# Node-score softmax turned through DRAM instead of TensorE, and x1 written over x

## The chip, the cores and the metric

The kernel runs on one core of one Trainium2 chip. The metric is device time in microseconds (us) of one launch. Before the change three runs took 2731.12, 2731.03 and 2728.78 us, so the median is 2731.03 us. All arithmetic is in float32.

## What is computed

The input is a batch of 64 graphs of 256 nodes with 512 features (x), their weighted adjacency matrices (256 x 256) and a node mask. Layer 0 is a three-step graph convolution with a residual and a layer norm; layer 1 is a graph attention in which each node gets one score, and the scores of a graph go through one softmax over its 256 nodes.

```python
x0 = relu(adj @ (x  @ W1) + b1)
x0 = relu(adj @ (x0 @ W2) + b2)
x1 = layernorm(x + adj @ (x0 @ W3) + b3)
q, k = split(x1 @ Wqk);  v = x1 @ Wv
w = sum_d(q * (adj @ (k * mask))) * mask / sqrt(512)      # one score per node
out = layernorm(x1 + softmax(w, over the 256 nodes)[:, None] * v)
```

## The kernel before, in words

The 64 graphs are worked on as 32 pairs (G = 2, NPAIR = 32). A graph's 256 nodes fill the 128 partitions twice (NH = 2 halves h). Every matrix product is done as seven smaller products of half-size blocks instead of eight (`seven`, L108), so each product needs sums and differences of blocks, made by VectorE (DVE), GpSimd (POOL) or ScalarE (ACT); `unit` (L65) chooses between DVE and POOL by the list ON_DVE (L36). One such product is seven steps on TensorE (PE).

A pair goes through these stages, each written as a Python generator that yields after every step:

- **F** (`front`, L416): x @ W1 (`support`, L293; matmuls at L301), adj times that (`aggregate`, L324; matmuls at L342), the same for W2, and x0 @ W3. In its course it issues the load of the next pair's transposed x (L73) and, near its end, of this pair's plain x (`load_x`, L85 to L90).
- **S** (`sums`, L426): the block sums of the next pair's transposed x (`a_sums` with the names x7, x6, x5, x3) and of its adjacency, and x + b3 (L437).
- **B** (`back`, L442): adj times (x0 @ W3) plus x (matmuls at L378), layer norm of the sum into x1 (called `r`), a masked copy `xm` (L471), and x1 transposed by 32 x 32 blocks on DVE (L498) and two DMA stages through DRAM (`via`, L502 and L504). In the last pair PE does this transpose (L487).
- **G** (`gather`, L512): adj times the masked x1 (L378).
- **M** (`attention`, L525): the 28 steps of x1 @ (Wq Wk^T) and x1 @ Wv (matmuls at L556), whose weights are fetched from DRAM through a ring of seven buffers (`fetch`, L221; DMA at L226), and the node scores: four instructions (L573) that multiply and sum along a row, each of which fills one column of the small tile `w` (128 partitions x 4 scores).
- **E** (`finish`, L604): the softmax of the scores, v * s + x1 (L613, four instructions), the second layer norm and the store (L634).

Pair i's stages run in three consecutive rounds of the outer loop (L667): F in round i, B, G and M in round i + 1, E in round i + 2. Within a round, a string of letters (ORDER; START, LAST and END for the first and last rounds) says which generator takes its next step. `manual_schedule` (L45) makes this the order of instructions on every engine's queue: no instruction passes another one of its own engine, and that holds for the DMAs too, which are all issued by SyncE (SP). In the trace the engine PE also shows as PEld, its weight loads, which run beside the matmuls.

The **softmax** is in `softmax_rows` (L390) and `softmax_cols` (L405). A softmax over nodes runs across partitions, so the scores are first turned: two PE transposes (L395) put the two graphs' scores as two rows of 256 into a PSUM bank. DVE takes the negated maximum (L397), ACT the exponential with its sum (L400, which makes ACT load another function table first), DVE the reciprocal and the product (L402, L403) into the tile `e_t`. Two PE matmuls with the identity (L409; each is two instructions in float32) turn the rows back to columns in another PSUM bank, and DVE copies them to the tile `s` (L412), which L613 reads. E's first step is up to L403, its second from L409 to L613.

**Buffers**: the tiles x and xm share one buffer (tag x) and r has its own (tag r); each is 8 KB on each of the 128 partitions. A tile that is given a buffer waits until the last reader of the tile before it is done. x1 of pair i (r) lives until L613 of round i + 2.

Of the kernel before, what the change touches and what calls it, by code (L numbers as in the profile page):

```python
# [9 lines left out]
FP = mybir.dt.float32  # L10
AF = mybir.ActivationFunctionType
OP = mybir.AluOpType
AX = mybir.AxisListType

P = 128
PAIR = 2
G = PAIR
# [3 lines left out]
def gcn_then_graph_attention(ctx: ExitStack, tc: tile.TileContext, xT, xN, adjT, mask, W1, b1, W2, b2, W3, b3,  # L21
                             WqT, WkT, Wv, out):

    nc = tc.nc
    NPAIR = xT.shape[0]
    N, D = 256, 512
    NH, DC = N // P, D // P
# [5 lines left out]
    SBUFS = 6  # L33
    SEEDS = 2
    TMP = 5
    ON_DVE = ('a3', 'a5', 'a6', 'a7', 'b3', 'c1T5', 'c1T6', 'c1T7', 'c2T5', 'c2T6', 'c2T7', 'c3T7', 'h17', 'h23', 'h25', 'h26', 'h27')  # L36

    const = ctx.enter_context(tc.tile_pool(name="const", bufs=1))
    pool = ctx.enter_context(tc.tile_pool(name="work", bufs=1))
    small = ctx.enter_context(tc.tile_pool(name="small", bufs=2))  # L40
    dram = ctx.enter_context(tc.tile_pool(name="dram", bufs=2, space=bass.MemoryType.DRAM))
# [5 lines left out]
    def bank(shape=(P, G, N)):  # L47
        return psum.tile(list(shape), FP, name="ps", tag="ps")
# [36 lines left out]
    def load_x(i):  # L85
        k = small.tile([P, NH, G], FP, name="mask")
        nc.sync.dma_start(k, mask[i].rearrange("p (h g) -> p h g", h=NH))
        t = pool.tile([P, G, NH, D], FP, name="x", tag="x", bufs=1)
        nc.sync.dma_start(t, xN[i].rearrange("p (g h f) -> p g h f", g=G, h=NH))
        return t, k  # L90

# [75 lines left out]
    ident = const.tile([P, P], FP, name="ident")  # L167
# [14 lines left out]
    begin, end = load_w(W1, 1, True)  # L182
# [5 lines left out]
    for n, b in ((1, b1), (2, b2)):  # L188
        t = const.tile([P, DC], FP, name=f"b{n}")
# [38 lines left out]

    def make_m():

        wq = pool.tile([P, DC, D], FP, name="wqT", tag="r", bufs=1)
        wk = pool.tile([P, DC, D], FP, name="wkT", tag="T", bufs=1)
        for d in range(DC):
            for t, w in ((wq, WqT), (wk, WkT)):
                nc.sync.dma_start(t[:, d], w[d * P:(d + 1) * P, :])
        m = pool.tile([P, 2, 2, D], FP, name="m", tag="v", bufs=1)
        v = pool.tile([P, 2, 2, D], FP, name="wv", tag="gt", bufs=1)
        nc.sync.dma_start(v, Wv.rearrange("(k c p) f -> p k c f", k=2, p=P))
        yield
        for f in range(DC):  # L240
            pt = bank((P, D))
            for d in range(DC):
                for j in range(DC):
                    nc.tensor.matmul(pt[:, j * P:(j + 1) * P], lhsT=wq[:, d, f * P:(f + 1) * P],
                                     rhs=wk[:, d, j * P:(j + 1) * P], start=(d == 0 and j == 0),
                                     stop=(d == DC - 1), skip_group_check=True)
            nc.scalar.copy(m[:, f // 2, f % 2, :], pt)
            yield
        t12 = pool.tile([P, 2, 2, D], FP, name="t12", tag="r", bufs=1)
        t34 = pool.tile([P, 2, 2, D], FP, name="t34", tag="T", bufs=1)  # L250
        sub = OP.subtract

        for o, a, b, op in ((t12[:, 0], v[:, 0], m[:, 0], sub), (t12[:, 1], m[:, 1], t12[:, 0], OP.add),
                            (t34[:, 0], m[:, 1], m[:, 0], sub), (t34[:, 1], v[:, 1], t12[:, 1], sub)):
            for c in range(2):
                nc.vector.tensor_tensor(o[:, c], a[:, c], b[:, c], op=op)
                yield
        B = {1: v[:, 0], 2: v[:, 1], 3: m[:, 1], 4: t34[:, 1], 5: t12[:, 0], 6: t12[:, 1], 7: t34[:, 0]}
        at = {n: k for k, n in enumerate(INNER)}
        for q, outer in enumerate(OUTER):  # L260
            for k, n in enumerate(outer):
                w = pool.tile([P, 7, HD], FP, name="w7", tag=("Za", "Ia")[place[n] % 2], bufs=1)
                blk = [B[n][:, c, j * HD:(j + 1) * HD] for c in range(2) for j in range(2)]
                for i, b in ((1, blk[0]), (2, blk[2]), (3, blk[3])):
                    nc.scalar.copy(w[:, at[i]], b)
                yield from b_steps(blk, [w[:, at[i]] for i in (5, 6, 7, 4)], nc.vector)
                nc.sync.dma_start(w_dram[q][:, :, k], w)
                yield
        for k in range(RING):
            fetch(k)  # L270
# [116 lines left out]
        nc.vector.reciprocal(rs, sd)  # L387
        return rs

    def softmax_rows(w, gs):  # L390

        n = len(gs)
        pw = bank((n, N))
        for h in range(NH):
            nc.tensor.transpose(pw[:, h * P:(h + 1) * P], w[:, h, gs[0]:gs[0] + n], ident)  # L395
        nmax = small.tile([n, 1], FP, name="nmax")
        nc.vector.tensor_reduce(nmax, pw, AX.X, OP.max, negate=True)  # L397
        e = e_t[:n]
        tot = small.tile([n, 1], FP, name="tot")
        nc.scalar.activation(e, pw, AF.Exp, bias=nmax, accum_out=tot)  # L400
        rtot = small.tile([n, 1], FP, name="rtot")
        nc.vector.reciprocal(rtot, tot)  # L402
        nc.vector.tensor_scalar(e, e, rtot, None, op0=OP.mult)  # L403

    def softmax_cols(gs):  # L405
        n = len(gs)
        ps = bank((P, NH, n))
        for h in range(NH):
            nc.tensor.matmul(ps[:, h, :], lhsT=e_t[:, h * P:(h + 1) * P], rhs=ident[:, :n],  # L409
                             start=(h == 0), stop=(h == NH - 1), skip_group_check=True)  # L410
        s = small.tile([P, NH, n], FP, name="s", bufs=2)
        nc.vector.tensor_copy(s, ps)  # L412
        return s
# [26 lines left out]
            yield from adj_sums(aTs[i + 1], put)  # L440

    def back(i, C, aS, x, mask_t, end, put):  # L442
        r = pool.tile([P, G, NH, D], FP, name="r", tag="xT" if end else "r", bufs=1)
        xb = lambda h, j: x[:, :, h, j * HD:(j + 1) * HD]
        rb = lambda h, j: r[:, :, h, j * HD:(j + 1) * HD]
        st = small.tile([P, NH, G, 6], FP, name="st")
# [14 lines left out]
        nc.vector.tensor_scalar(ms, mask_t, ISCALE, None, op0=OP.mult)  # L461
        rs = inv_std(mvt)
        yield
        xm = pool.tile([P, G, NH, D], FP, name="xm", tag="x", bufs=1)

        def turn(h, g):
            nc.vector.tensor_scalar(r[:, g, h, :], r[:, g, h, :], mvt[:, h, g, 0:1], rs[:, h, g:g + 1],
# [51 lines left out]
                        aTs[i + 2] = load_adj(i + 2)  # L519
                yield  # L520
        put["G"] = gather()
        w = small.tile([P, NH, G], FP, name="w", bufs=2)
        put["M"] = attention(i, x1b, w, r, mask_t, put)

    def attention(i, x1b, w, r, mask_t, put):  # L525
# [45 lines left out]
        def score(R, h, g):  # L571
            t = put["gt"][:, h, g, :]
            nc.vector.scalar_tensor_tensor(t, R[:, g].rearrange("p j f -> p (j f)"), mask_t[:, h, g:g + 1], t,  # L573
                                           op0=OP.mult, op1=OP.mult, accum_out=w[:, h, g:g + 1])

        def results(g):

# [26 lines left out]
    def finish(i, prev, gs=range(G)):  # L604

        r, v, w = prev
        n = len(gs)
        softmax_rows(w, gs)
        yield
        s = softmax_cols(gs)  # L610
        for k, g in enumerate(gs):
            for h in range(NH):
                nc.vector.scalar_tensor_tensor(v[:, g, h], v[:, g, h], s[:, h, k:k + 1], r[:, g, h, :],  # L613
                                               op0=OP.mult, op1=OP.add)
        yield
        st = small.tile([P, NH, n, 6], FP, name="st")
        mvt = small.tile([P, NH, n, 2], FP, name="mvt")
        for k, g in enumerate(gs):
            for h in range(NH):
                nc.vector.bn_stats(st[:, h, k], v[:, g, h])  # L620
                yield
        for k in range(n):
            for h in range(NH):
                nc.vector.bn_aggr(mvt[:, h, k], st[:, h, k])  # L624
        rs = inv_std(mvt, n)
        nb = small.tile([P, NH, n], FP, name="nb")
        nc.vector.scalar_tensor_tensor(nb, mvt[:, :, :, 0], -1.0, rs, op0=OP.mult, op1=OP.mult)  # L627
        yield
        for k, g in enumerate(gs):
            for h in range(NH):  # L630
                nc.scalar.activation(v[:, g, h], v[:, g, h], AF.Identity, scale=rs[:, h, k:k + 1],  # L631
                                     bias=nb[:, h, k:k + 1])
                yield
            nc.sync.dma_start(out[i, :, g * NH * D:(g + 1) * NH * D].rearrange("p (h f) -> p h f", h=NH), v[:, g])  # L634

    ORDER = ("BBFEFFBBEFBBFBFBFFFFFBFFFFBFBBBFFFBFSEBGGFSGGEFEEGFMSGMFMGMFMFMFMMMEMMFMFMMMSMFEEESM"
             "SMEMFEFSEFMMMFMSMMMMSMMMMMMMMSMMMMSMMMF")
    START = ("BBFFFFFBBFFBBBBBFFFFFFFBBBBBFSFBBBBSBBBFBBBBBFBBBBBBBFBBFFFFFFBSFFFFSBBBBBBFSFBFBSBS"
             "BBFBBSFSSBSBBBBBBBBBBBFBBBSBB")
    LAST = ("FFBEBFBBEBBFFBSFBFFFEFFBSFSFFBFBFFBBFBBEEFGEEEGFGGFGFMMFMGFMFMFGMFMEEMMMMFMFFMMMSSEM"  # L640
            "SMSFMSEMMFSFMMMMMEMFMMMMMMMMMMFMMSMMMSM")
    END = ("BBBBBBBBBBBEBBBBGGEMGGMEMBGEEEBGMMMMEMMMMEMEMMEEEBMMMMMMGMMMMMMMMMMMMMMMMXMMXXMMXYMX"
           "YMYXMXMXYXYMMXMMYYYYXYYMXMY")

    def run(order, rest, **gens):
        res = {}
# [81 lines left out]
```

## Time and profile before

| | us |
|---|---|
| median of the three runs | 2731.03 |
| the profiled execution | 2725.27 |
| its span (first to last instruction) | 2723.5 |
| time around the span (difference of these two) | 1.77 |
| PE busy | 2694.6 |
| DVE busy | 2118.6 |
| ACT busy | 1278.4 |
| POOL busy | 925.5 |

The mean granted clock of TensorE was 0.996. The DMA queues moved 403.72 MB.

How to read the views that follow. In the *timeline* each row is a start in us from the start of the span, a duration, an engine, a source line, an operation with what it writes and reads, and how many instructions the row joins; a bracket at the end gives the engine's idle time before it and what ended that. PE instructions are pipelined, so a row overlaps the next one: the cost of a row of matmuls is the distance from its start to the start of the next row. In the *waits* a row names the instruction that waited and what it waited for, and then the sum in us, the number of times, and the longest. In the list of *DMA issues* the last number is the median time in us from issue to landing. "The order" is the sequence of instructions on each engine in the built program, with their waits; it has no times in it.

### The profile page before, as it was taken

Reading aid. Unit: us, or ns where it says so; the run is one execution under the profiler, and the core shown is the slowest. Engines: PE = TensorE matmul, PEld = TensorE weight load, DVE = VectorE, ACT = ScalarE, POOL = GpSimd, SP = SyncE. Lnnn points to the kernel's source line nnn. Section 1 sums busy time; section 2 is a strip of 40 time slices with the busy share of each in tenths; the row PEclk is TensorE's granted clock in tenths of the full one; section 3 lists DMA queues with packets and bytes.
Section 4 is the critical chain, followed back from the end, with each engine's and each line's share of the span. In section 5 each row is a group of like instructions: output and inputs, shape, how many; then the busy total and the mean of one; then the engine's idle time right before and its main releaser. Section 6 shows DMA issues by size and latency. Waiting matters only on the chain. (4 is left out here: it accounts for less than half of the span.)

```text
span 2723.5 us, 41056 instructions
## 1 busy us (share of the span) xinstructions
PE 2694.6 (99%) x14306; PEld 2410.4 (89%) x14306; DVE 2118.6 (78%) x3700; ACT 1278.4 (47%) x2338; POOL 925.5 (34%) x678
## 2 busy tenths in 40 slices
PE   9999999999999999999999999999999999999996
PEld 8888888888898888888888988889888889888885
DVE  5777777878777887777787778877787877787777
ACT  3534455444554444454444554444544445444444
POOL 2422343322434223433224442234332244322332
PEclk9999999999999999999999999999999999999998
DMA  5534554345544445543455444455434454444552
GB/s 199 170 123 149 165 166 137 123 149 162 165 140 131 137 149 165 174 136 116 152 158 165 142 132 136 146 164 178 135 117 152 154 164 148 136 132 146 160 157 99
DMA packets 202235, 403.72 MB, mean 148 GB/s; under 512 B 24752, under 2 KB 61872, under 8 KB 193968
## 3 DMA queue, kind: packets, MB, share of 16 engines
q1 hardware_dynamic: 202032, 401.10, 46.8%
q8 instruction: 117, 1.92, 0.3%
q14 instruction: 86, 0.70, 0.1%
HBM read 328.54 MB, written 72.48 MB: 147 GB/s over the span
## 5 line engine op out<-in xcount | busy, mean ns | idle before, releaser
L556 PE MATMUL ps<-ring,I 128*128 128x256 f32 x1792 | 434.8, 380 | 3.4 <-DVE seed L57 1.8
L66 POOL TENSOR_TENSOR S<-hT,S 128x512 f32<-128x512 f32 x64 | 93.1, 1454 | 1005.3 <-DVE S L66 1005.3
L556 PEld LDWEIGHTS ps<-ring,I 128*128 128x128 f32 x1792 | 332.5, 190 | 47.3 <-issue 4.4
L301 PE MATMUL ps<-w_T,S 128*128 128x256 f32 x1536 | 352.5, 379 | 0.0
L113 ACT COPY tmp<-ps 128x512 f32<-128x512 f32 x512 | 287.2, 588 | 123.3 <-PE ps L301 60.9
L301 PEld LDWEIGHTS ps<-w_T,S 128*128 128x128 f32 x1536 | 289.1, 190 | 39.4
L122 ACT COPY seed<-ps 128x512 f32<-128x512 f32 x256 | 146.1, 571 | 307.9 <-PE ps L301 167.4
L66 POOL TENSOR_TENSOR sup<-sup 128x512 f32<-128x512 f32 x64 | 81.8, 1298 | 589.3 <-DVE sup L66 589.3
L57 DVE TENSOR_TENSOR sup<-ps,tmp 128x512 f32<-128x512 f32 x192 | 131.5, 685 | 156.4 <-PE ps L301 155.9
L301 PE MATMUL ps<-w_T,hT 128*128 128x256 f32 x1024 | 236.7, 379 | 0.0
L63 POOL TENSOR_TENSOR I<-Z 128x384 f32<-128x384 f32 (+1 forms) x128 | 191.0, 1513 | 123.5 <-DVE Z L537 105.0
L66 DVE TENSOR_TENSOR sup<-sup 128x512 f32<-128x512 f32 x224 | 219.5, 981 | 10.3 <-DVE sup L57 0.5
L556 PE MATMUL ps<-ring,Z 128*128 128x256 f32 x896 | 219.5, 379 | 0.0
L301 PEld LDWEIGHTS ps<-w_T,hT 128*128 128x128 f32 x1024 | 194.6, 190 | 26.5
L57 DVE TENSOR_TENSOR R<-ps,tmp 128x512 f32<-128x512 f32 (+1 forms) x256 | 153.4, 621 | 74.2 <-PE ps L556 65.9
L342 PE MATMUL ps<-aS,sup 128*128 128x128 f32 x1536 | 203.3, 279 | 0.0
L342 PEld LDWEIGHTS ps<-aS,sup 128*128 128x128 f32 x1536 | 193.4, 191 | 10.4 <-DVE hT L57 2.0
L342 PEld LDWEIGHTS ps<-aT,sup 128*128 128x128 f32 x1536 | 194.4, 192 | 6.6
L342 PE MATMUL ps<-aT,sup 128*128 128x128 f32 x1536 | 199.3, 276 | 0.0
L556 PEld LDWEIGHTS ps<-ring,Z 128*128 128x128 f32 x896 | 167.7, 190 | 21.8 <-DVE tmp L57 0.4
L301 PE MATMUL ps<-w,S 128*128 128x256 f32 x768 | 182.8, 381 | 2.5 <-DVE sup L57 2.5
L565 ACT COPY R<-seed 128x512 f32<-128x512 f32 (+1 forms) x128 | 66.5, 545 | 242.0 <-PE seed L556 242.0
(135 smaller groups left out, 5407.2 us busy)
## 6 DMA issues: line engine op xcount, KB each, us to landing
ring<-mv SPq DMA_DIRECT2D x672, 256.0 KB, 3.5
x<-in_xN SPq DMA_DIRECT2D x32, 1024.0 KB, 5.2
out<-v SPq DMA_DIRECT2D x64, 512.0 KB, 3.5
xT<-in_xT SPq DMA_DIRECT2D x31, 1024.0 KB, 4.8
via<-tr SPq DMA_DIRECT2D x31, 1024.0 KB, 4.2
x1T<-via SPq DMA_DIRECT2D x124, 256.0 KB, 4.6
ring<-mv SPq DMA_DIRECT2D x224, 128.0 KB, 2.7
aT<-in_adjT SPq DMA_DIRECT2D x32, 512.0 KB, 3.6
```

The costliest lines, as they stand in the source:

```text
L57: nc.vector.tensor_tensor(o, a, b, op=OP.add)
L63: (nc.gpsimd).tensor_tensor(o, a, b, op=op)
L66: (nc.vector if name in ON_DVE else nc.gpsimd).tensor_tensor(o, a, b, op=op)
L113: nc.scalar.copy(t, ps)
L122: nc.scalar.copy(y, x)
L301: nc.tensor.matmul(ps[:, g], lhsT=src[n][:, c, g], rhs=w[n][:, c], start=(first and g == 0 and c == 0), stop=(g == G - 1 and c == 1), skip ...
L342: nc.tensor.matmul(ps[:, c, g], lhsT=C[n][:, g, c * P:(c + 1) * P], rhs=aS[n][:, g], start=(first and c == 0 and g == 0), stop=(c == 1 and ...
L556: nc.tensor.matmul(ps[:, k], lhsT=left[n](place[o]), rhs=wt[:, k], start=(first and k == 0), stop=(k == len(outer) - 1), skip_group_check= ...
L565: return seven(mm, (P, len(outer), HD), lambda y: nc.scalar.copy(R[:, :, 0, 0], y), c12, lambda v, t: add(R[:, :, 1, 0], v, t), lambda v, ...
```

## The change

For the first 31 pairs (the last pair's graphs are finished one at a time and keep the PE path) the softmax no longer uses PE or PSUM. The scores are written from `w` to DRAM, element by element in row order (`wr`), read back as two rows of 256 (`row`), put through the same softmax in place, written to DRAM again (`sr`), and read back as columns into `s`. E gains steps for this: one for each of the four DMAs and one for the row arithmetic. The tile `w` changes its order from (h, g) to (g, h) so that the DMA's pattern is plain.

x1 is written in place over x (r = x), the tag r goes, and tag x has two buffers; xm takes its buffer from tag x too (in the last pair from tag xT). The two set-up tiles that used tag r use tag x.

Two of the block sums after x @ W1 (names c1T5 and c1T6) move from DVE to POOL, and one sum of x (x3) from POOL to DVE. The four strings ORDER, START, LAST and END are new, so the order of instructions differs throughout.

```diff
-    ON_DVE = ('a3', 'a5', 'a6', 'a7', 'b3', 'c1T5', 'c1T6', 'c1T7', 'c2T5', ...
+    ON_DVE = ('a3', 'a5', 'a6', 'a7', 'b3', 'c1T7', 'c2T5', ... 'x3')
...
-        t = pool.tile([P, G, NH, D], FP, name="x", tag="x", bufs=1)
+        t = pool.tile([P, G, NH, D], FP, name="x", tag="x", bufs=2)
...
-    def softmax_rows(w, gs):
-
-        n = len(gs)
-        pw = bank((n, N))
-        for h in range(NH):
-            nc.tensor.transpose(pw[:, h * P:(h + 1) * P], w[:, h, gs[0]:gs[0] + n], ident)
+    def softmax_rows(src, e):
+
+        n = e.shape[0]
         nmax = small.tile([n, 1], FP, name="nmax")
-        nc.vector.tensor_reduce(nmax, pw, AX.X, OP.max, negate=True)
-        e = e_t[:n]
+        nc.vector.tensor_reduce(nmax, src, AX.X, OP.max, negate=True)
         tot = small.tile([n, 1], FP, name="tot")
-        nc.scalar.activation(e, pw, AF.Exp, bias=nmax, accum_out=tot)
+        nc.scalar.activation(e, src, AF.Exp, bias=nmax, accum_out=tot)
...
+    def turned(w):
+
+        flat = dram.tile([G, N], FP, name="wr", bufs=2)
+        nc.sync.dma_start(flat.rearrange("g (h p) -> p (g h)", h=NH), w.rearrange("p g h -> p (g h)"))
+        yield
+        row = small.tile([G, N], FP, name="row", bufs=1)
+        nc.sync.dma_start(row, flat)
+        yield
+        softmax_rows(row, row)
+        yield
+        flat = dram.tile([G, N], FP, name="sr", bufs=2)
+        nc.sync.dma_start(flat, row)
+        yield
+        s = small.tile([P, G, NH], FP, name="s", bufs=2)
+        nc.sync.dma_start(s.rearrange("p g h -> p (g h)"), flat.rearrange("g (h p) -> p (g h)", h=NH))
+        yield
+        return s.rearrange("p g h -> p h g")
...
-        r = pool.tile([P, G, NH, D], FP, name="r", tag="xT" if end else "r", bufs=1)
+        r = x
...
-        xm = pool.tile([P, G, NH, D], FP, name="xm", tag="x", bufs=1)
+        xm = pool.tile([P, G, NH, D], FP, name="xm", tag="xT" if end else "x", bufs=1 if end else 2)
...
-        softmax_rows(w, gs)
-        yield
-        s = softmax_cols(gs)
+        if n == G:
+            s = yield from turned(w)
+        else:
+            pw = bank((n, N))
+            for h in range(NH):
+                nc.tensor.transpose(pw[:, h * P:(h + 1) * P], w[:, gs[0], h:h + 1], ident)
+            softmax_rows(pw, e_t[:n])
+            yield
+            s = softmax_cols(gs)
...
-    ORDER = ("BBFEFFBBEFBBFBFBFFFFFBFFFFBFBBBFFFBFSEBGGFSGGEFEEGFMSGMFMGMFMFMFMMMEMMFMFMMMSMFEEESM"
-             "SMEMFEFSEFMMMFMSMMMMSMMMMMMMMSMMMMSMMMF")
+    ORDER = ("BBEEFFFBBEFFEBEBFBFFEFBFFFFFFFBBBSFBFEFBBBGGFEGFGEGFGEMFFGMSMFMMFMEMFFMSMMMFMMESMFME"
+             "EEMMSSEMFMFSMMMMFFMMMMMSMSEMMMMMMMMMMSSFMMM")
```

More of the change, by code (lines that the diff above doesn't have):

```diff
@@ L35, in gcn_then_graph_attention @@
     TMP = 5
-    ON_DVE = ('a3', 'a5', 'a6', 'a7', 'b3', 'c1T5', 'c1T6', 'c1T7', 'c2T5', 'c2T6', 'c2T7', 'c3T7', 'h17', 'h23', 'h25', 'h26', 'h27')
+    ON_DVE = ('a3', 'a5', 'a6', 'a7', 'b3', 'c1T7', 'c2T5', 'c2T6', 'c2T7', 'c3T7', 'h17', 'h23', 'h25', 'h26', 'h27', 'x3')
     const = ctx.enter_context(tc.tile_pool(name="const", bufs=1))
@@ L229, in make_m @@
     def make_m():
-        wq = pool.tile([P, DC, D], FP, name="wqT", tag="r", bufs=1)
+        wq = pool.tile([P, DC, D], FP, name="wqT", tag="x", bufs=2)
         wk = pool.tile([P, DC, D], FP, name="wkT", tag="T", bufs=1)
@@ L248, in make_m @@
             yield
-        t12 = pool.tile([P, 2, 2, D], FP, name="t12", tag="r", bufs=1)
+        t12 = pool.tile([P, 2, 2, D], FP, name="t12", tag="x", bufs=2)
         t34 = pool.tile([P, 2, 2, D], FP, name="t34", tag="T", bufs=1)
@@ L521, in back @@
         put["G"] = gather()
-        w = small.tile([P, NH, G], FP, name="w", bufs=2)
+        w = small.tile([P, G, NH], FP, name="w", bufs=2)
         put["M"] = attention(i, x1b, w, r, mask_t, put)
@@ L573, in score @@
             nc.vector.scalar_tensor_tensor(t, R[:, g].rearrange("p j f -> p (j f)"), mask_t[:, h, g:g + 1], t,
-                                           op0=OP.mult, op1=OP.mult, accum_out=w[:, h, g:g + 1])
+                                           op0=OP.mult, op1=OP.mult, accum_out=w[:, g, h:h + 1])
         def results(g):
@@ L634, in finish @@
             nc.sync.dma_start(out[i, :, g * NH * D:(g + 1) * NH * D].rearrange("p (h f) -> p h f", h=NH), v[:, g])
-    ORDER = ("BBFEFFBBEFBBFBFBFFFFFBFFFFBFBBBFFFBFSEBGGFSGGEFEEGFMSGMFMGMFMFMFMMMEMMFMFMMMSMFEEESM"
-             "SMEMFEFSEFMMMFMSMMMMSMMMMMMMMSMMMMSMMMF")
[L638 to L643, printed above, removed]
+    ORDER = ("BBEEFFFBBEFFEBEBFBFFEFBFFFFFFFBBBSFBFEFBBBGGFEGFGEGFGEMFFGMSMFMMFMEMFFMSMMMFMMESMFME"
+             "EEMMSSEMFMFSMMMMFFMMMMMSMSEMMMMMMMMMMSSFMMM")
+    START = ("FFFBFBBFBFBBFBBBFFFFFFFBBBBFBBSBSFBBBBFBBBBBBBBBBBFBFFBFFFBBSFBFFFBBFBFBBSBBFBFSFBBB"
+             "BBBSFSFSBSBBBSBBSBBBFBBBBSBBB")
+    LAST = ("EFFBFBBBESEEEFBBFFBFFEBFFFFFFBFFBFBFBFBBBEEFFEGSFGGEEFGGMFGMGFEMMMFFMEFMMMSMFFMSMSMS"
+            "FEMMEMESMSMMSMFMFMMMMMFMEMSMMMMMMMSMFMMMMMM")
+    END = ("BBBBBBBBBBEBEEEEBBBBGGMMBMGGGGMMMEMEMEMMBEEMEMMEMEEEEMMBMMMMMMMGMMMMMMMMMMMMMXMMXMXM"
+           "MXMYXYXMMYXYXYYXYXYYYYYMXXMMMMM")
     def run(order, rest, **gens):
```

## Prediction

> **What bounds the kernel now.** First the busy times of the page, then the waits of TensorE.
>
> ```profile
> PE 2694.6 (99%) x14306; PEld 2410.4 (89%) x14306; DVE 2118.6 (78%) x3700; ACT 1278.4 (47%) x2338; POOL 925.5 (34%) x678
> ```
>
> ```profile
> PE ps L409 <- DVE e_t L403: 4.4, 3, 2.1
> PE ps L395 <- DVE gt L573: 4.1, 2, 3.1
> PE ps L301 <- DVE sup L57: 2.5, 1, 2.5
> PE ps L378 <- DVE seed L57: 2.3, 1, 2.3
> ```
>
> PE is busy for 2694.6 of 2723.5 us, and the waits it has come one to three times in the whole run, not once in each of the 32 pairs: they belong to the first and last rounds or to single pairs. In a normal pair PE runs without a pause that the profile counts. So PE sets the time, and an instruction taken from PE is won in full, as long as nothing new makes PE wait. A stretch of PE's timeline around one pair's softmax gives the price.
>
> ```profile
> 1242.24 1.89 PE L301 MATMUL ps<-w,xT 128*128 128x256 f32 x8
> 1243.97 0.38 PE L395 MATMUL ps<-ident,w 128*2 128x128 f32 x2
> 1244.19 3.62 PE L301 MATMUL ps<-w_T,S 128*128 128x256 f32 x16
> ...
> 1249.37 0.50 PE L409 MATMUL ps<-ident,e_t 128*128 128x2 f32 x4
> 1249.73 1.97 PE L301 MATMUL seed<-w,xT 128*128 128x256 f32 x8
> 1251.54 1.89 PE L378 MATMUL ps<-sup,aT 128*128 128x256 f32 x8
> ```
>
> Eight matmuls of 256 columns take 1243.97 - 1242.24 = 1.73 us from start to start. The two transposes take 1244.19 - 1243.97 = 0.22, the four matmuls of L409 1249.73 - 1249.37 = 0.36, and the eight behind them 1251.54 - 1249.73 = 1.81 instead of 1.73, so 0.08 more is L409's doing. Together **0.66 us per pair**.
>
> **The change part by part.**
>
> *1. The PE instructions that go.* 31 pairs x 0.66 = **-20.5 us**. The reader should see that the mean durations of the page (276 ns for a transpose, 237 ns for L409) would say 2 x 0.276 + 4 x 0.237 = 1.5 us, because they count pipelined ends twice.
>
> *2. The round trip that comes.* It lies beside PE's work if its last transfer lands before DVE reaches the four L613. I count from 1242.24, the start of the first row above. DVE's rows:
>
> ```profile
> 1242.34 0.08 DVE L573 DVE_READ_ACCUMULATOR gt<-R,mask,gt 128x1 f32 x1
> ...
> 1244.48 0.40 DVE L397 TENSOR_REDUCE nmax<-ps 2x1 f32<-2x256 f32 x1
> 1246.70 0.15 DVE L402 RECIPROCAL rtot<-tot 2x1 f32<-2x1 f32 x1 [1.82 <-ACT e_t L400]
> 1246.88 0.34 DVE L403 TENSOR_SCALAR e_t<-e_t,rtot 2x256 f32<-2x256 f32 x1
> 1248.71 1.29 DVE L57 TENSOR_TENSOR tmp<-ps,x 128x512 f32<-128x512 f32 x2 [1.48 <-PE ps L378]
> ```
>
> The last score is there at +0.2, so wr can be issued then. In the new order the maximum stands behind the pair of tmp sums, which begin at 1248.71 and end at 1250.00, or +7.5 with the transposes gone. wr and row have 7.3 us. The arithmetic took 1247.22 - 1244.48 = 2.7 us, table load included, and nothing in it depends on where the row lies, so it ends at +10.3. sr and s follow. The L613 stand in the new order behind the last subtraction of x @ W1 (L60). That cannot begin before +17.0 (PE ends its product at 1259.31 - 0.66, which is +16.4, and ACT copies it first, about 0.6), and stood at +19.0 before. Adding the pitches of what DVE must do from PE's product at +12.1 on (four sums at 0.6, two pairs of statistics at 1.4, one sum of sup at 0.7) I put its end at +18.2. So sr and s have **7.9 us**.
>
> What a transfer costs is bounded by the rows of DMA issues:
>
> ```profile
> via<-tr SPq DMA_DIRECT2D x31, 1024.0 KB, 4.2
> x1T<-via SPq DMA_DIRECT2D x124, 256.0 KB, 4.6
> mask<-in_mask SPq DMA_DIRECT2D x32, 2.0 KB, 2.2
> ```
>
> Each new transfer moves 2 KB, as the mask does: 2.2 us. The upper end is the kernel's own round trip through DRAM, 4.2 out and 4.6 back. I take 2.2 plus 0.4 for issuing each (the length of an issue in SP's timeline): 5.2 us for a pair of transfers, 2.7 inside what sr and s have, so **0 us**. At the upper end, 8.8 + 0.8 = 9.6, s comes 1.7 late.
>
> The page "DMA: Bandwidth & Descriptors" of the Trainium skill speaks against this (section "Rules for kernel authors"): a non-contiguous last dimension becomes one descriptor per element, and a transpose by a rearranged access pattern is to be avoided, with a 19-fold difference. wr and s are such patterns, 512 single elements each, where the mask's are 128 runs. If that factor held for the 2.2 us, each would take an estimated 42 us, DVE would stand still in every pair, and the kernel would be about twice as slow. No row here moves single elements, so the trace cannot refute it; I go by the row with the same bytes.
>
> *3. What queues behind the new waits.* On SP the four DMAs stand between the last ring fetch and the load of xT:
>
> ```profile
> 1228.19 11.15 SPq L226 DMA_DIRECT2D ring<-mv  x14
> 1257.83 0.33 SPq L73 DMA_DIRECT2D xT<-in_xT  x1
> ```
>
> SP is idle from 1239.34 to 1257.83. It issues s at about +13.3 (10.3, then 2.6 for sr, 0.4), and xT is due at +15.6, since it waits for PE; the next ring fetch comes 30 us later. **0 us**; it would take 2.3 us more per transfer of the second half to delay xT, whose first use (POOL, 1276.92) has 14 us to spare. On ACT the exponential, with its table load, waits for the row; a tmp copy and a sup copy stand behind it. On DVE the maximum waits for the row, and what stands behind it needs a PE product that ends at +10.4. Up to 2 us of lateness there is covered.
>
> *4. In place over x, two buffers.* Before, ACT waited 135.2 us in 30 waits to write r until L613 had read the old one; that goes, but PE never waited for it: **0**. Memory is the same (x and r before, two x after). The load of x still waits in the new order for ACT and POOL to be done with xm, and DVE's 37.0 us in 31 waits for x never reached PE. If it did after the change, 1.2 us per pair would be lost; if it ends, PE has nothing to win: 0.
>
> *5. Block sums.* Two sums at 0.7 leave DVE (POOL takes 1.3 each) and one of 0.7 comes (POOL took 1.65). POOL is at 34%. The second adjacency block that PE takes from POOL's sum is due at +18.2 by PE's count and ready at about +16.9: **0**, bounds -0.1 and +0.6 us per pair.
>
> *6. The new order.* It can't be priced from the trace of before. Two places are tight. With L613 (2.7 us) now late, the sum into hT that PE waits for ends at about +21.7, and PE wants its bank at +21.8; and four layer-norm steps with their transposes instead of three now follow, so via leaves about 0.7 us later against PE's need. Before, PE lost 0.34 us there: 1265.92 - 1259.31 = 6.61 for 56 matmuls at 0.112. Bounds per pair: all of the 0.34 won back (-10 us in all), or twice as much lost (+20). I take 0.13, **+4 us**.
>
> *7. The ends.* The last round keeps PE's softmax for its two graphs, but the pair before them now has L613 behind the sums of z instead of ahead of them. Before, those four took 3.79 us of DVE there while PE paused and then ran for some 3 us at half pitch (2672.59 to 2676.06). I take **-2 us**, bounds -6 and +4. First round: 0, bounds -2 and +2.
>
> Sum: -20.5 + 4 - 2 = -18.5, against the profiled execution: 2725.27 - 18.5 = 2706.8 (its span 2723.5 and 1.8 around it). The median of the three runs is 5.8 above that execution, which I add: **2712 us**, 0.7% faster.
>
> **The rivals.**
>
> *The transfers come late (slower).* Behind L613 there is almost no slack before PE (point 6), so each us that s lands after +18.2 costs PE about one us per pair. The break-even is 0.66 + 0.13 less, about 0.5 us late, that is sr and s together 8.4 us instead of 5.2. At the round trip's own 9.6 us: 31 x 1.7 = +53, less 18.5: about 2765 us. For it: single elements, and writes that must have landed in DRAM before they are read. Against: the 2.2 us of the same bytes, and a DMA queue that is empty there.
>
> *Half of the win goes into new waits.* If the two tight places of point 6 cost 0.35 us more per pair than I took: +11, 2723 us. For it: slack of under 1 us at several places, worked out from rows of another order. Against: DVE has less to do than before.
>
> *Nothing moves.* If DVE's chain and not PE were what holds a pair, taking PE work away would only show as PE idle: 2731. Against: waits that come one to three times in 32 pairs.
>
> *More is won.* Tail and the 0.34 go as well: 2731 - 33 = 2698.
>
> **How the numbers follow.** Forecast 0.62; late transfers 0.10; half lost 0.18; nothing 0.05; more 0.05. A measurement of this kernel tells about 0.2% (5.5 us) from no change. Half lost is at the border, so 0.10 of it counts as faster and 0.08 as the same. Faster: 0.62 + 0.10 + 0.05 = 0.77. Same: 0.08 + 0.05 = 0.13. Slower: 0.10. The range takes in the forecast, nearly all of half lost, and part of more: 2698 to 2726.
>
> **What would show it.** Right: no rows of L395 and L409 but for the last pair; PE busy about 20 us less; DVE's waits list with no, or under 0.3 us per pair, wait of the maximum for row or of L613 for s; a pair 0.5 to 0.7 us shorter. Wrong: wr and s with 4 us or more to landing, DVE's L613 waiting for s in each pair, and PE waiting 31 times in the sums into hT (L342) or for Z and I (L556).

## The result and the profile after

The changed kernel takes **2874.58 us** (median of 5 runs, 2871.81 to 2876.72) against 2730.51 us for the kernel before in the same session (5 runs, 2728.78 to 2731.12): ratio 1.0529, 95% interval [1.0513, 1.0544]. The forecast was 2712, the range 2698 to 2726. It is 144 us slower where 19 us less were expected.

I read the page of the changed kernel in the order in which the prediction read the one of before: first the busy times, then TensorE's waits.

```profile
PE 2734.7 (95%) x14120; PEld 2421.0 (84%) x14120; DVE 2086.0 (73%) x3637; ACT 1264.1 (44%) x2338; POOL 959.0 (33%) x710
```

```profile
PE ps L301 <- ACT tmp L113: 103.8, 30, 4.6
PE ps L423 <- DVE e_t L399: 4.6, 2, 2.7
PE ps L627 <- DVE gt L587: 3.8, 2, 2.6
```

The 186 small instructions are gone (14306 before, 14120 now), but PE's share fell from 99% to 95%, and at the top of its waits (total, times, longest) stands one that comes 30 times: the matmuls of L301 wait for a bank that ScalarE's copy at L113 has to empty. It was not there before. The waits of the other engines say why ScalarE is late.

```profile
DVE nmax L394 <- DMA row<-wr: 171.2, 30, 6.8
ACT L396 <- DMA row<-wr: 168.1, 30, 6.7
...
SPq L407 <- DMA wr<-w: 276.7, 31, 10.9
SPq L412 <- DVE row L399: 162.1, 31, 5.8
...
SPq L415 <- DMA sr<-row: 25.6, 31, 0.9
```

L407, L412 and L415 are the issues of row, sr and s (that of wr is L404). The issue of row waits 8.9 us for wr in each pair; the maximum (L394) and the exponential (L396) then wait another 5.6 to 5.7 us for the row (5.54 and 5.44 in the pair shown below). The issue of s waits only 0.8 us for sr, and L633, which needs s, isn't in the list at all. So the first half of the round trip is late and the second is not. One pair in the timeline, queue by queue (SP, then ScalarE with VectorE's maximum, then PE; columns are start, length, instruction, and in brackets the idle time ahead of it with what ended it):

```profile
1218.45 0.37 SPq L404 DMA_DIRECT2D wr<-w  x1
1227.10 0.25 SPq L407 DMA_DIRECT2D row<-wr  x1
1233.24 0.25 SPq L412 DMA_DIRECT2D sr<-row  x1
1234.40 0.39 SPq L415 DMA_DIRECT2D s<-sr  x1
```

```profile
1224.73 0.59 ACT L470 COPY x<-seed 128x512 f32<-128x512 f32 x1 [1.14 <-PE seed L378]
1230.69 0.41 DVE L394 TENSOR_REDUCE nmax<-row 2x1 f32<-2x256 f32 x1 [5.54 <-DMA row<-wr]
1230.76 1.28 ACT L396 ACT_TABLE_LOAD   x1 [5.44 <-DMA row<-wr]
1232.06 0.51 ACT L396 ACTIVATE row<-row,nmax 2x256 f32<-2x256 f32 x1
1232.47 0.18 ACT L396 ACTIVATION_READ_ACCUMULATOR row<-row,nmax 2x1 f32 x1
1232.56 0.56 ACT L113 COPY tmp<-ps 128x512 f32<-128x512 f32 x1
```

```profile
1219.35 3.62 PE L301 MATMUL ps<-w_T,S 128*128 128x256 f32 x16
...
1226.26 1.89 PE L301 MATMUL ps<-w_T,xT 128*128 128x256 f32 x8
1227.98 1.89 PE L378 MATMUL ps<-sup,aT 128*128 128x256 f32 x8
1233.17 3.78 PE L301 MATMUL ps<-w_T,xT 128*128 128x256 f32 x8 [3.30 <-ACT tmp L113]
1236.74 1.91 PE L378 MATMUL ps<-sup,aS 128*128 128x256 f32 x4
```

wr is issued at 1218.45 and seen to have landed at 1227.10, 8.65 us later. The row then takes until 1230.7. ScalarE takes its instructions in order, and the copy of L113 stands behind the exponential. It copies the product of step 7 (`out(v, 2)` in `seven`), the first half of the sixteen matmuls of 1219.35, so what it reads was there long before; PE needs its bank for step 4 and stops for 3.30 us. Then it runs at half speed: eight matmuls take 1236.74 - 1233.17 = 3.57 us, where the prediction's rows of before had 1.73. Counting, over the whole trace, how far PE's starts stand apart beyond 216 ns (256 columns) or 112 ns (128 columns): 211 us in after, 40 in before. 105 us of it are the 29 pauses between L378 and L301, 30 the slow matmuls straight behind them, about 12 the next ones. 171 more, less some 20 for the work that went, make the 151.4 us between the two spans (2874.9 and 2723.5).

### The profile page after: what moved, and what is told of

It is laid out like the page before. It is cut to its first block, busy times and chain, and to the rows that moved or that the text cites. A ratio compares the mean times of both kernels' runs of the same rounds, so it can differ in the third digit from the quotient of the medians.

```text
span 2874.9 us, 40725 instructions
## 1 busy us (share of the span) xinstructions
PE 2734.7 (95%) x14120; PEld 2421.0 (84%) x14120; DVE 2086.0 (73%) x3637; ACT 1264.1 (44%) x2338; POOL 959.0 (33%) x710
## 5 line engine op out<-in xcount | busy, mean ns | idle before, releaser
L66 POOL TENSOR_TENSOR sup<-sup 128x512 f32<-128x512 f32 x128 | 161.3, 1282 | 1337.4 <-DVE sup L66 1168.4
L113 ACT COPY tmp<-ps 128x512 f32<-128x512 f32 x512 | 286.8, 588 | 228.2 <-PE ps L301 134.3
L301 PE MATMUL ps<-w_T,S 128*128 128x256 f32 x1536 | 352.4, 379 | 0.0
L301 PEld LDWEIGHTS ps<-w_T,S 128*128 128x128 f32 x1536 | 291.5, 190 | 40.1
L63 POOL TENSOR_TENSOR I<-Z 128x384 f32<-128x384 f32 (+1 forms) x128 | 205.8, 1627 | 283.2 <-DVE Z L551 179.2
L301 PE MATMUL ps<-w_T,xT 128*128 128x256 f32 x512 | 152.3, 450 | 103.8 <-ACT tmp L113 103.8
L301 PE MATMUL ps<-w_T,hT 128*128 128x256 f32 x1024 | 236.5, 379 | 0.0
L312 ACT COPY sup<-ps 128x512 f32<-128x512 f32 x96 | 56.3, 586 | 380.8 <-PE ps L301 367.8
L301 PEld LDWEIGHTS ps<-w_T,xT 128*128 128x128 f32 x512 | 111.1, 222 | 133.3 <-ACT tmp L113 115.8
L301 PEld LDWEIGHTS ps<-w_T,hT 128*128 128x128 f32 x1024 | 194.6, 190 | 26.5
L342 PEld LDWEIGHTS ps<-aT,sup 128*128 128x128 f32 x1536 | 193.7, 192 | 14.7 <-issue 6.7
L342 PE MATMUL ps<-aS,sup 128*128 128x128 f32 x1536 | 200.9, 279 | 3.9 <-DVE hT L57 3.7
L342 PE MATMUL ps<-aT,sup 128*128 128x128 f32 x1536 | 200.4, 277 | 1.7
L342 PEld LDWEIGHTS ps<-aS,sup 128*128 128x128 f32 x1536 | 186.6, 192 | 13.5 <-DVE hT L57 7.9
L301 PE MATMUL ps<-w,S 128*128 128x256 f32 x768 | 185.4, 385 | 3.3 <-DVE sup L57 3.3
```

The costliest lines, as they stand in the source:

```text
L63: (nc.gpsimd).tensor_tensor(o, a, b, op=op)
L66: (nc.vector if name in ON_DVE else nc.gpsimd).tensor_tensor(o, a, b, op=op)
L113: nc.scalar.copy(t, ps)
L301: nc.tensor.matmul(ps[:, g], lhsT=src[n][:, c, g], rhs=w[n][:, c], start=(first and g == 0 and c == 0), stop=(g == G - 1 and c == 1), skip ...
L312: nc.scalar.copy(C[2], x)
L342: nc.tensor.matmul(ps[:, c, g], lhsT=C[n][:, g, c * P:(c + 1) * P], rhs=aS[n][:, g], start=(first and c == 0 and g == 0), stop=(c == 1 and ...
```

## The experiments

**Theory 1**: the 512 single elements that wr writes to DRAM land late, and ScalarE's queue hands the lateness to TensorE. **Theory 2**: the new order, x1 in place of x, or the moved sums cost the time. **Theory 3**: any round trip through DRAM costs this, whatever its pattern. Each time is a median, with its ratio to the kernel before run beside it.

**e1_runs: the same transfers, wr in runs of 16 bytes.**

```
-  dma_start(flat.rearrange("g (h p) -> p (g h)", h=NH), w...)
+  dma_start(flat.rearrange("g (q c) -> (g q) c", c=G * NH), w...)
```

> One line of the kernel after is changed: wr writes each partition's four scores as one run of 16 bytes (128 runs) in place of 512 single elements; same bytes, same four transfers, same order. The scores of a row are then those of mixed nodes and graphs, so what the softmax runs over is not the reference's. Theory 1 (the single elements that wr writes are what lands late): wr to row shrinks from about 9 us to 4 us or less, the row no longer comes 5.5 us after VectorE, and most of the 105 us of pauses ahead of L301 goes: about 2760 us, and about 2715 if row's own landing shrinks too. Theory 2 (the order, the in-place x1 or the moved sums cost the time): no change, 2875. Theory 3 (any write to DRAM that is read back takes this long, whatever its pattern): no change, 2875, with wr to row still at about 9 us.

Measured 2718.69 us, 0.9961 [0.9946, 0.9976]. One line takes 156 us off. The rows of e1 mix nodes and graphs, so it doesn't compute the layer; e8 and e9 below do, in the same time. wr to row's issue is 1.59 us (median of 31; 1.44 to 1.46 in the three other kernels with this write) instead of 8.92. SP's wait for wr and the first two of TensorE's waits in e1:

```profile
SPq L407 <- DMA wr<-w: 43.2, 31, 2.3
```

```profile
PE ps L423 <- DVE e_t L399: 4.6, 2, 2.7
PE ps L627 <- DVE gt L587: 3.6, 2, 2.5
```

The wait for L113 is gone from the list, and so is any wait for the row. Theory 1 had said 2760, or 2715 if the row came sooner too; it is the second. Theories 2 and 3 had said 2875 and fall.

**e3_pe_both: the new order, x1 in place and the sums, with TensorE's transposes and matmuls instead of the four transfers.**

```
   def turned(w):
...
+      for h in range(NH):
+          nc.tensor.transpose(pw[:, h * P:(h + 1) * P], w[:, :, h], ident)
+      softmax_rows(pw, e_t[:G])
...
+      return softmax_cols(range(G))
```

> The kernel after with its order, its in-place x1 and its block sums, but with no transfer: TensorE transposes the scores ahead of the softmax and turns them back with four matmuls, at the same places of the order. Theories 1 and 3 (the transfers cost all of it): about 2731 us, as before. Theory 2 (order, in-place or sums): about 2875 plus the 20 us of TensorE's work, 2890.

2729.36 us, 0.9998 [0.9989, 1.0008]: everything in the change but the transfers, taken together, is worth nothing either way. Theory 2 falls a second time, and the prediction's points 4 and 5 (0) and 6 with 7 (+4 and -2) hold within the interval.

**e4_pe_in: TensorE turns the scores into rows, only sr and s go through DRAM.**

```
+  for h in range(NH):
+      nc.tensor.transpose(pw[:, h * P:(h + 1) * P], w[:, :, h], ident)
+  row = small.tile([G, N], FP, name="row", bufs=1)
+  softmax_rows(pw, row)
...  (sr and s as in after)
```

> Half of the change: TensorE transposes the scores into rows, as before, and only the way back (sr and s) goes through DRAM. It saves the 0.36 + 0.08 us of L409's four matmuls in each of 31 pairs. If the way back is as well covered as the trace of after shows (no wait of L633 for s): 2731 - 14 = about 2717 us, order aside. If every round trip through DRAM of this kind costs what the first one does: over 2800.

2724.92 us, 0.9985 [0.9975, 0.9994]. The second half through DRAM costs no wait, as expected, but it brings 4 us, not 14; the last experiments ask why.

**e6c_late: all transfers as in after, the softmax later in the order**, behind the tmp and sup copies on ScalarE. Only the letters of ORDER change.

```
-  "BBEEFFFBBEFFEBEBFBFFEFBFFFFFFFBBB...
+  "BBEEFFFBBFFBBEFEEBFFFEBFFFFFFFBBB...
```

> The kernel after with all its transfers, but the softmax of the row (maximum, exponential, scaling) is taken later in the order: behind the first pair of statistics on VectorE, behind the two copies on ScalarE that stood behind the exponential. L633 keeps its place. Theory 1 with the place as cause (an instruction that waits in ScalarE's in-order queue holds copies that TensorE needs): the pauses ahead of L301 go and the waits shrink to what is still late, 2710 to 2745 us. If instead the latency itself is on the path wherever the wait stands, the loss moves to L633 and the time stays near 2860.

2757.02 us, 1.0108 [1.0092, 1.0123]. The latency is still there, and TensorE pays little of it: the three top waits of e6c and the one for L113, with SP's wait for wr as long as in after.

```profile
PE ps L342 <- DVE hT L57: 20.7, 29, 0.7
PE ps L342 <- POOL sup L66: 6.6, 29, 0.5
PE ps L423 <- DVE e_t L399: 4.6, 2, 2.7
...
PE ps L301 <- ACT tmp L113: 3.5, 1, 3.5
```

```profile
SPq L407 <- DMA wr<-w: 277.2, 31, 10.7
```

116 of the 144 us go with the place of the softmax in the queues. It moved on VectorE and ScalarE alike; that ScalarE's queue was the one that mattered is read from the wait for L113, which is gone but for one. What remains is new: the maximum, its scaling and 0.7 us of waiting for the exponential now stand on VectorE ahead of the sums that L342 needs, and L342's waits come to 27 us. The forecast (2710 to 2745) was 12 us short at its upper end. The place and the latency are both causes: neither alone costs the 144 us.

**e2_gather: the single elements moved from the write to the read.**

```
+  dma_start(flat.rearrange("g (q c) -> (g q) c", c=G * NH), w...)
...
+  for h in range(NH):
+      dma_start(row[:, h * P:(h + 1) * P], by_node[:, h:h + 3:NH].rearrange("p g -> g p"))
```

> The single elements are moved from the write to the read: wr is written as 128 runs of 16 bytes, and the row is gathered from it in 512 single elements, by two transfers (one for each half of a row). Same bytes through DRAM, one transfer more. Theory 1 in its narrow form (single elements are slow where they are written to DRAM, and not where they are read, as s showed): wr to row about 1.6 us as in e1, the row in time or up to 1.5 us late for the second issue, 2715 to 2735 us. Wide form (any pattern of single elements is slow): near 2875, with row itself taking 8 us or more.

2720.20 us, 0.9967 [0.9955, 0.9979]. Reading 512 single elements from DRAM in two transfers costs nothing that shows; writing them is what costs.

**e8_pairs: another order of the nodes in a row.** A row's maximum and sum don't care for the order of its nodes, so a node's two scores may stand side by side; wr is then 256 runs of 8 bytes.

```
-  dma_start(flat.rearrange("g (h p) -> p (g h)", h=NH), w...)
+  dma_start(flat.rearrange("g (p h) -> p g h", h=NH), w)
...
-  dma_start(s..., flat.rearrange("g (h p) -> p (g h)", h=NH))
+  dma_start(s, flat.rearrange("g (p h) -> p g h", h=NH))
```

> The kernel after with the nodes of a row in another order: a node's two scores stand side by side, so wr writes 256 runs of 8 bytes in place of 512 of 4, and s reads 256 runs of 8. The sum and the maximum of a row don't depend on the order, and s reads in the order in which wr wrote, so the reference is computed. Theory 1 with a price per run: e1 (128 runs) had 1.59 us from wr's issue to row's, after (512 runs) 8.92, so 19 ns for a run; 256 runs land after about 4.0 us, the row stands some 0.5 us later than VectorE wants it, and the time is 2718 to 2730 us. A price by size of the run (anything under some size as slow as 4 bytes): near 2875.

2719.08 us, 0.9960 [0.9946, 0.9973]: **the change with two access patterns altered beats both kernels**, by 10 us the one before and by 155 the one it was made from. wr to row's issue is 3.16 us, less than the 4.0 worked out from a price per run. The same pair in e8 shows no gap: the exponential starts 0.03 us after the copy before it (ScalarE's rows), and TensorE goes from group to group without a bracket.

```profile
1162.66 0.58 ACT L470 COPY x<-seed 128x512 f32<-128x512 f32 x1 [1.14 <-PE seed L378]
1163.27 1.28 ACT L396 ACT_TABLE_LOAD   x1
```

```profile
1165.92 1.89 PE L378 MATMUL ps<-sup,aT 128*128 128x256 f32 x8
1167.64 1.89 PE L301 MATMUL ps<-w_T,xT 128*128 128x256 f32 x8
1169.37 1.03 PE L378 MATMUL ps<-sup,aS 128*128 128x256 f32 x4
```

**e9_pairs_read: wr in 16-byte runs, row read in 8-byte runs.**

```
+  dma_start(flat.rearrange("g (q c) -> (g q) c", c=G * NH), w...)
...
+  dma_start(row.rearrange("g (p h) -> g p h", h=NH), flat.rearrange("a (q g h) -> g (a q) h", g=G, h=NH))
...  (s as in e8)
```

> wr written as 128 runs of 16 bytes (as e1), the row read from it in 256 runs of 8 bytes, s read in runs of 8 bytes; the order of the nodes in a row is that of e8, the reference is computed. Theory 1: as e1, about 2719 us, as long as reads of 8 bytes cost no more than 1 us over the row's contiguous read. This is the change as it was meant, without element writes, and should beat the kernel before by about 10 us.

2719.79 us, 0.9966 [0.9953, 0.9978], as e1 and e8: whether row can be issued 1.45 or 3.16 us after wr makes no difference that shows.

**e11_pad: is it the number of runs or their size?** Each score in 8 bytes, 512 runs.

```
+  w = small.tile([P, G, NH, 2], FP, name="w", bufs=2)
+  nc.gpsimd.memset(w, 0.0)
...
+  dma_start(flat.rearrange("g (h p) c -> p (g h) c", h=NH), w.rearrange("p g h c -> p (g h) c"))
...
+  dma_start(row, flat[:, :, 0])
```

> The kernel after with every score padded to 8 bytes: wr writes 512 runs of 8 bytes (4 KB in all), in the node order of after, and the row is read in 512 single elements, which e2 showed to cost nothing here; one small memset on POOL in each pair. It tells the number of runs from their size. If the price is one per run, whatever its size (after: 512 runs, 8.92 us): wr to row about 9 us and the time near 2875. If runs of 4 bytes cost more than runs of 8 (e8: 256 runs of 8 in 3.16 us, so 512 would take about 6.3): the row some 2.7 us earlier than in after, of the 3.4 us that TensorE pauses in each pair about 0.7 stay, and the time is 2745 to 2790.

2729.81 us, 1.0003 [0.9994, 1.0012], faster than either expectation. The waits of SP's queue for wr, in e8 (256 runs of 8 bytes) and in e11 (512 of 8), beside the 276.7 us of after (512 of 4):

```profile
SPq L407 <- DMA wr<-w: 90.8, 31, 4.1
```

```profile
SPq L407 <- DMA wr<-w: 106.6, 31, 4.5
```

Twice the runs cost 0.8 us more (3.16 and 3.95 us from issue to issue), half the size 5.0 more (3.95 and 8.92). So the price is not one per run: runs of 4 bytes are a case of their own. The second expectation was right that the size counts; both took the number of runs as the measure, and there both fall. e11 is some 11 us slower than e8. Its row still comes up to 2.9 us late on VectorE (38.0 us in 29 waits, 1.3 on average); how much of the 11 us is this, and how much the added memset on GpSimd, no run tells apart.

**e10_split: why 10 us and not 20?** e9, with the softmax's scaling two sums later on VectorE.

```
+      tot = softmax_rows(row, row)      # maximum and exponential
       yield
+      scale_rows(row, tot)              # reciprocal and scaling
+      yield
...
```

> e9, with the softmax cut in two: maximum and exponential at their place, the reciprocal and the scaling two sums later in VectorE's order, so that VectorE does those sums while ScalarE loads its table and takes the exponential (1.8 us of waiting in each pair of e1). What is to be told: in e1 TensorE lost 10.6 us more than before in L342's matmuls, by waits under 0.25 us. If they come from VectorE's lateness after the softmax, this kernel wins most of them back: about 2710 us. If they come from elsewhere (L633 ahead of the hT sums, ScalarE or POOL), it stays at e9's time.

2719.01 us, 0.9965 [0.9953, 0.9978]: as e9. But VectorE's wait only changed its place, and so e10 decides nothing. The first of the sums that it should have done meanwhile waits for the copy of L315, and that stands behind the exponential on ScalarE. VectorE's waits for it in e9 and in e10:

```profile
DVE sup L57 <- ACT sup L315: 13.5, 29, 0.5
```

```profile
DVE sup L57 <- ACT sup L315: 80.7, 29, 2.8
```

The 67 us more take the place of the 56.0 us for which e9's reciprocal (L398) waits for the exponential.

**e12_sd_late: the layer norm's square root behind the tmp copies on ScalarE.**

```
-  "BBEEFFFBBEFFEBEBFBFFEFBFFFFFFFBBB...
+  "BBEEFFFBBEFFEBEBFBFFEFFFBFFFFFBBB...
```

> e8, with the standard deviation of the layer norm (L385, a table load of 1.28 us and the square root) moved behind the two tmp copies on ScalarE that free TensorE's banks in L342. In e8 TensorE loses 9.9 us in L342's matmuls that it did not lose before, most of it 0.22 us in each pair ahead of the third group, which comes just after the first of these copies. If ScalarE's table load ahead of the copies is the cause: 0.22 x 31 = 7 us less, about 2712 us. If VectorE (L633 ahead of the hT sums) is the cause, no gain, 2719, or some us more because the reciprocal behind L633 now waits for the later standard deviation.

2760.14 us, 1.0111 [1.0098, 1.0125]. TensorE's first wait in e12:

```profile
PE ps L342 <- DVE hT L57: 45.7, 30, 1.8
```

The reciprocal (L387), which VectorE has ahead of the sums into hT, now waits for the later square root, and TensorE behind them for 1.5 us a pair. The gain that was looked for is there all the same, but smaller than this new wait: see e14.

**e13_v_late: L633 behind the sums into hT.**

```
-  "BBEEFFFBBEFFEBEBFBFFEFBFFFFFFFBBB...
+  "BBEEFFFBBEFFEBEBFBFFBFFFFFEFFFBBB...
```

> e8, with the four L633 (2.73 us of VectorE, waiting for s) moved behind the two sums into hT and the sum of S that follows them. If L633 ahead of the hT sums is what TensorE waits for in L342: up to 7 us less, about 2712 us. If ScalarE's table load is the cause: no gain at that place, 2719, unless the later L633 delays the transposes of x1 and what follows.

2954.15 us, 1.0824 [1.0809, 1.0838], the slowest of all. Its first wait on TensorE, and the wait of ScalarE that grew with it (36.6 us in e8, from which e13 was made):

```profile
PE ps L301 <- ACT tmp L113: 163.7, 29, 5.7
```

```profile
ACT xm L485 <- DVE x L481: 224.6, 122, 6.1
```

It is the mechanism of after with another cause: on ScalarE the scaling of xm (L485) waits for VectorE, a copy of L113 stands behind it, and TensorE stops for 5.6 us in each pair. No transfer is late here. And one thing that the expectation asked is answered: the wait of 0.22 us inside L342 is as long in e13 as in e8 (222 ns in 32 of 33 places in both), so L633 is not its cause.

**e14_sd_split: e12, with the reciprocal behind the sums into hT as well.**

```
+  nc.scalar.activation(sd, mvt[:, :, :, 1], AF.Sqrt, bias=eps)
+  yield
+  nc.vector.reciprocal(rs, sd)
...  (and the letters of ORDER, LAST and END for the added step)
```

> e12 with its new wait taken away: the standard deviation (L385 in e12) stays behind the two tmp copies on ScalarE, and the reciprocal of it moves behind the sums into hT on VectorE, where e12 left it ahead of them, so that they waited (TensorE: 45.7 us in 30 waits of L342 for hT). e12's small waits were gone: its 128-column matmuls without those pauses stood 115.2 ns apart, e8's 117.6, before's 114.9. So 2.4 ns x 3712 = about 9 us less than e8: 2710 us, if ScalarE's table load was the cause. If the pitch was only hidden by e12's pauses, 2719 as e8.

2748.28 us, 1.0065 [1.0053, 1.0077]. At its place the cause is right. These are the rows of e8 there (ScalarE, then TensorE):

```profile
1173.69 1.28 ACT L385 ACT_TABLE_LOAD   x1
1174.99 0.30 ACT L385 ACTIVATE sd<-mvt,eps 128x4 f32<-128x4 f32 x1
1175.19 1.05 ACT L113 COPY tmp<-ps 128x512 f32<-128x512 f32 x2
```

```profile
1174.79 1.06 PE L342 MATMUL seed<-aT,sup 128*128 128x128 f32 x8
1175.90 2.02 PE L342 MATMUL ps<-aT,sup 128*128 128x128 f32 x16
```

The sixteen of 1175.90 follow the eight before them by 1.11 us, where eight matmuls at 112 ns take 0.90. This start comes 222 to 223 ns late in e8, e1 and e4 (median of 32 places), and 36 ns in e14 and 37 in e12, where the square root stands behind the copies. But two other groups now wait, in every pair of e14:

```profile
1193.99 3.69 PE L301 MATMUL ps<-w_T,S 128*128 128x256 f32 x16 [0.29 <-DVE rs L480]
...
1199.71 1.97 PE L301 MATMUL ps<-w_T,hT 128*128 128x256 f32 x8 [0.30 <-ACT tmp L113]
```

0.45 us each, 28 us in all, against the 6 won. ScalarE's table load has to stand somewhere among copies that TensorE waits for. Both other places that were tried cost more than the first, so what an ideal order would give stays open.

## Why the prediction was wrong

**The step that failed is point 2's price of a transfer**: "Each new transfer moves 2 KB, as the mask does: 2.2 us". It was applied to four transfers. For wr that is less than a third of what it took: 8.92 us from its issue to that of row (512 single elements written to DRAM), against 2.2 + 0.4. The row, contiguous, takes 3.4 instead of 2.2. Together 12.4 us, where 5.2 were taken and 7.3 were there: 5 us of lateness. In the pair shown it is 12.24 of 6.70, or 5.54; the last score ended 0.8 us into the pair and not 0.2, which takes 0.6 from the 7.3. sr and s stayed inside what they have. sr's landing took 1.15 us from issue to issue, and s, 512 single elements written to SBUF, was there for L633 in e6c within 2.8 us. So the same price was right for s and wrong for wr; what tells them apart is that wr's elements are written to DRAM, and s's (as row's in e2) read from it.

The bounds had the same fault. The upper end, the kernel's own round trip of 4.2 and 4.6 us, was called the upper end though no row of the trace wrote elements. wr took more than twice that. A bound has to come from a row of the same kind, or be left open upward.

**The skill's rule** that was set aside (DMA: Bandwidth & Descriptors, "Rules for kernel authors") pointed at wr and at s alike: wr was slow, though the 42 us are too high for it by a factor of nearly five, and s was not. It doesn't fit as a count of descriptors: e2 reads 512 single elements from DRAM without a wait of TensorE, and e11 writes 512 runs of 8 bytes in 3.95 us. Only writes of 4 bytes to DRAM showed the high price.

**Point 3** had the queue right and its size too: "a tmp copy and a sup copy stand behind it [...] Up to 2 us of lateness there is covered". The row was 5.54 us late on VectorE and TensorE stopped for 3.30, so 2.2 us were covered. What it left out is the price beyond that cover: the other 3.3 us are TensorE's, and behind the stops come slow matmuls, (30 + 12) / 29 = 1.4 us in a pair.

**The slower rival** had the right sign and the wrong place. It let s come late at L633 and gave 2765 us, with a chance of 0.10. What came late was the row, through ScalarE's queue. Point 2 gave the first pair of transfers 7.3 us and the second 7.9, so the first had the smaller margin, and no rival was built on it.

**Points 4, 5, 6 and 7** hold together: e3 differs from before by half a us, inside its interval, where their sum was +2. e3 doesn't tell them apart, so they may be wrong singly.

**Point 1** was 1.7 us too high. Summed over the trace of before, from each start to the next, the 62 transposes and the 124 small matmuls make 6.8 + 12.0 = 18.8 us, not 20.5.

**The rival "half of the win goes into new waits"** is what the change is worth without its slow write: e8 gives 2719.08 (that rival said 2723, the forecast 2712). L342's matmuls stand 118.0 ns apart in e8, 115.3 in before and 115.7 in e3 (mean of the distances under 400 ns); 2.7 ns x 3584 = 10 of the 18.8 us are given back in small waits. They come as soon as L409's matmuls leave (e4: 118.0). The 0.36 us of PE work there had covered ScalarE's table load for the square root, which delays the copies that empty L342's banks. For the largest of these waits, 7 of the 10 us, e12 and e14 show that the table load is the cause, and e13 that L633 is not; for the others, and for what had covered it before, it is argued.

## What to carry to other kernels

A small transfer is priced by where it writes and in what runs, not by its bytes alone: an access pattern of single elements is put on the side that reads DRAM, or the data's order is chosen so that runs of 8 bytes or more are written, as a softmax allows. A wait is priced by what stands behind it in its engine's order: the same late row cost 155 us ahead of a copy that TensorE needs (after against e8) and 38 behind it (e6c against e8). Work taken off the busiest engine is won only where nothing else had been hiding under it; here half of it had.

## What the runs showed of the hardware

- Time from issuing the write to issuing the read that depends on it, medians of 31: 128 runs of 16 bytes 1.59 us (e1), 256 runs of 8 bytes 3.16 (e8), 512 runs of 8 bytes 3.95 (e11), 512 runs of 4 bytes 8.92 (after). The packet records don't show it: a packet of 4 bytes is recorded with 7 to 9 ns as one of 8 or 16 is, and in the pair shown wr's packets are all recorded by about 1220, 7 us before the landing. e11 also spreads its elements over twice the memory. Whether 4 bytes is the threshold, or something else in how such writes meet in memory, was not tried.
- TensorE's granted clock (third column from the end) in four stretches around after's pause: before it, in it, and two behind it.

```profile
1224.00:1230.00 6.00, 5.87 (x28) 4.82 (x26) 1.15 (x2) 0.59 (x1) 0.00 (x0) 1.00 0.00 0
1230.00:1233.10 3.10, 0.00 (x0) 0.00 (x0) 0.79 (x3) 2.33 (x5) 0.00 (x0) 0.83 0.01 3
1233.10:1236.70 3.60, 3.53 (x8) 2.86 (x9) 3.44 (x8) 0.50 (x2) 0.00 (x0) 0.50 0.07 1
1236.70:1240.30 3.60, 3.60 (x13) 2.96 (x12) 2.96 (x5) 0.00 (x0) 1.58 (x2) 0.70 0.66 203
```

The clock's records in after's trace have it at 0.50 from 1232.02, still in the stop of 3.3 us, to 1238.85, and the matmuls of 256 columns stand 427 ns apart until 1238.45. Each such stretch behind a stop lasted 3.41 us or twice that, and all falls of the clock in after, and all in e13, lie whole multiples of 3.41 us apart. Of after's 29 stops (2.8 to 4.6 us) 22 brought one and 7 did not; e13's 29 stops of 5.6 us all did, e12's 30 of 1.5 us none. Nine of after's 11 stops shorter than 3.41 us brought one, and 5 of the 18 longer ones did not, so at this length the length of a stop alone doesn't decide it. e12's stops left the mean pitch of 256 columns at 216.9 ns, e13's raised it to 223.5. The Trainium skill's page "TensorE: Matmul & The Clock Gate" (Part 1: The HAM clock gate) gives half speed after an idle window of about 3.4 us. The stretches of 3.41 us fit that; but in the pair shown the clock fell 2.15 us after the last matmul before the stop had ended, so an idle time of 3.4 us was not needed here.
